# Cross-attention block: one 512-column V product per head group, one ring of eight PSUM banks, a rewritten order

## The chip, the core and the metric

The kernel runs on one core of a Trainium2 chip. The metric is the device time of one execution in microseconds; lower is better. The median of three runs before the change is 760.53 us (760.25 to 760.59).

PE is the matrix engine, with PEld for its weight loads; DVE, ACT and POOL are the vector, scalar and GpSimd engines; SP issues most of the DMAs. SBUF is the on-chip memory of the operands. PSUM holds what PE writes, in eight banks of 512 float32 values per partition.

## The reference

B = 4 batches, 512 queries and 512 context rows of width D = 512, H = 16 heads of HD = 32, a hidden layer of 2048, all in float32:

```python
x = layer_norm(hidden_states, ln1_w, ln1_b)
q = (x @ q_w + q_b).reshape(B, LQ, H, HD).transpose(0, 2, 1, 3)
k = (encoder_hidden_states @ k_w + k_b)...   # likewise, and v
scores = einsum('bhqd,bhkd->bhqk', q, k) / sqrt(HD)
scores = where(mask, scores, finfo.min)
out = einsum('bhqk,bhkd->bhqd', softmax(scores), v)
hidden = out.reshape(B, LQ, D) @ cproj_w + cproj_b + hidden_states
y = gelu(layer_norm(hidden, ln2_w, ln2_b) @ fc_w + fc_b)
return hidden + y @ proj_w + proj_b
```

## The kernel before

Everything is laid out transposed, with features on the partitions. The attention runs in 16 groups w = 0 to 15, four per batch; a group is four heads, 128 features. One more idea shapes the second half: the hidden layer's products are split into quarters by a Strassen-like scheme (sums on POOL and DVE, fewer products on PE).

The order of all work is written out by hand in the string ORDER. Each token names a generator; each time the token stands in the string the generator runs up to its next `yield`, and what it issues is appended to the engines' queues in that order. No scheduler moves anything afterwards; every engine works through its own queue, and waits where an operand or a buffer is not ready. The tokens that matter here:

- `k:w`, `q:w`, `v:w` make a group's K, Q and V: four products of 128x512 on all 128 rows and columns of the array (V: sixteen of 128x128), then ACT moves the result out of PSUM.
- `u:w:t` (`scores`, L510) is a *score unit*: four products, one per head, each on 32 rows of the array and all 128 columns, for 128 queries t against 512 keys. The four lie side by side in the array's rows and write four banks.
- `x:w:t` (`exps`, L518 and L521) takes the four banks in turn: DVE adds the mask, copies to SBUF and takes the minimum; ACT takes exp and its sum.
- `r:w:t` (`turn`, L529 to L539) transposes the tiles in 32x32 blocks on DVE into a buffer `tb`; `d` (`stay`, POOL) and `e` (`exchange`, twelve DMAs on SP) move the blocks to their partitions in the buffer `pT`. There are two `tb` and two `pT`, one for each half of the queries.
- `a:w:half` (`attend`, L568) is the *V product*: for 4 key tiles and 4 heads, sixteen products with all 128 rows and 32 columns of the array; four heads lie side by side in the columns. Each streams 256 columns, the queries of one half. DVE then multiplies by the reciprocal sums (L574).
- `c:b:t` is the output projection (L443), `s2`, `r2`, `n2`, `t2`, `y` the second layer norm and its sums, `f:b:c` the first hidden product (L621), `j` its joins on ACT and DVE (L646, L651, L330), `g` the gelu, `P`, `pj`, `J` the second hidden product with its joins, `so` the stores of the result, `lc`, `lx`, `lf`, `wk`, `wq`, `wv` loads.

A float32 product shows in the trace as two matmul records, so a score unit has 8 records, a V product 32, a K product 8. I call a row of products that use the array in the same shape a *stretch*: full-array (k, q, v, c, f, P and the transposes), score (32 rows) or V (32 columns).

PSUM before is divided: four banks `sc` belong to the score units, four banks `acc` go round in a ring (class Ring: `take` pops the bank that came free first, `done` appends it) for all other products. In the last batch's hidden layers, when the scores are over, half of the results go to `sc` instead.

Of the kernel before, what the change touches and what calls it, by code (L numbers as in the profile page):

```python
# [20 lines left out]
P = 128  # L21
# [5 lines left out]
NG = ND  # L27
# [33 lines left out]
s1:0 k:0 s1:0 s1:0 s1:0 r1:0 n1:0 n1:0 n1:0 n1:0 wq:1 wv:1 k:0 v:0 k:1 k:1 qb t1:0:1 t1:0:1 t1:0:0 t1:0:3 t1:0:0  # L61
  t1:0:2 m:0 t1:0:2 t1:0:3 q:0 q:0
u:0:0 x:0:0 x:0:0 x:0:0 x:0:0 q:1 r:0:0
u:0:1 r:0:0 lx:1 lf:0:0 lf:0:0 wq:2 wv:2 v:1 wk:3 wk:2 lx:1 lx:1 lc wv:3 lf:0:2 v:0 x:0:1 x:0:1 x:0:1 x:0:1 r:0:1
  r:0:1 q:1
u:0:2 r:0:1 r:0:1 q:2 x:0:2 x:0:2 x:0:2 x:0:2
u:0:3 r:0:2 x:0:3 x:0:3 v:1 x:0:3 v:3 x:0:3
u:1:0 k:3 v:2 e:0:0 e:0:0 e:0:0 lh:0 lh:0 wq:3 r:0:2 r:0:3 r:0:3 lx:1 wv:5 m:0 d:0:0 v:1 d:0:0 x:1:0 s1:1 r:0:3 r:0:3
  e:0:1 e:0:1 e:0:1 v:3 s1:1 x:1:0 x:1:0 x:1:0 r:1:0 r:1:0
u:1:1 k:2 x:1:1 x:1:1 x:1:1 v:2 x:1:1 k:2 r:1:1 s1:1  # L70
u:1:2 r:1:1 q:2 s1:1 x:1:2 x:1:2 x:1:2 x:1:2 k:3 d:0:1 d:0:1 v:0 fs:0:0 r:1:2 r:1:1 q:3
u:1:3 r1:1 a:0:0 ts:1 r:1:1 x:1:3 ts:1 le:1 wk:4 wq:4 wk:5 lt:1 lt:1 le:1 le:1 le:1 a:0:1 a:0:0 x:1:3 e:1:0 ts:1 k:4
  r:1:2 r:1:3 x:1:3 x:1:3 k:4
u:2:0 k:5 r:1:3 x:2:0 x:2:0 a:0:1 k:5 x:2:0 x:2:0 r:1:3
u:2:1 r:1:3 x:2:1 e:1:0 lb:1 e:1:0 lb:1 lt:1 lt:1 lf:0:1 wq:5 wk:6 wv:4 cb:0 d:1:0 v:2 d:1:0 d:1:1 x:2:1 q:3 r:2:0 v:5
  a:1:0 x:2:1 r:2:1 x:2:1
u:2:2 r:2:0 x:2:2 x:2:2 x:2:2 x:2:2 r:2:1 r:2:1 a:1:0 v:4
u:2:3 r:2:1 v:4 x:2:3 x:2:3 k:6 e:1:1 e:1:1 e:1:1 e:2:0 e:2:0 e:2:0 wv:7 d:1:1 na:1 wa:1 na:1 r:2:2 x:2:3 x:2:3 r:2:3
  r:2:3 wa:1 na:1 wa:1 na:1 d:2:0 a:1:1
u:3:0 r:2:2 k:6 wa:1 x:3:0 a:1:1 x:3:0 x:3:0 x:3:0 r:2:3 r:2:3 q:5  # L80
u:3:1 x:3:1 v:5 wv:6 e:2:1 e:2:1 e:2:1 wk:7 wq:7 d:2:0 r:3:0 q:5 x:3:1 x:3:1 x:3:1 v:5 d:2:1 r:3:0 r:3:1 r:3:1 r:3:1
  d:2:1 cb:0 v:3 a:2:0 v:7
u:3:2 q:4 x:3:2 x:3:2 x:3:2 x:3:2 q:4 a:2:0 r:3:1 lf:0:3 e:3:0 e:3:0 e:3:0
u:3:3 a:2:1 q:7 r:3:2 x:3:3 x:3:3 x:3:3 x:3:3
u:4:0 k:7 d:3:0 d:3:0 a:2:1 r:3:2 r:3:3 r:3:3 m:1 r:3:3 r:3:3 x:4:0 x:4:0 x:4:0 x:4:0
u:4:1 r:4:0 v:7 x:4:1 x:4:1 x:4:1 v:6 e:3:1 e:3:1 wv:9 e:3:1 lf:0:2 x:4:1 v:6
u:4:2 r:4:0 r:4:1 a:3:0 x:4:2 x:4:2 k:7 r:4:1 a:3:0 x:4:2 r:4:1 r:4:1 x:4:2 c:0:1 d:3:1 v:4 d:3:1
u:4:3 r:4:2 c:0:0 a:3:1 x:4:3 x:4:3 q:7 x:4:3 c:0:1 r:4:3 x:4:3 c:0:0
u:5:0 r:4:2 r:4:3 x:5:0 x:5:0 a:3:1 x:5:0 x:5:0 c:0:2
u:5:1 c:0:3 s2:0 r:4:3 wk:8 lh:0 d:4:0 cb:0 c:0:2 s2:0 s2:0 r:4:3 le:2 lx:2 le:2 lf:0:1 wq:6 s1:2 wk:9 lh:0 e:4:0  # L90
  e:4:0 e:4:0 le:2 le:2 c:0:0 v:7 fs:0:0 fs:0:0 cb:0 d:4:0 fs:0:1 x:5:1 c:0:3 fs:0:0 m:1 v:6 c:0:1 d:4:1 e:4:1 q:6
  wv:8 e:4:1 e:4:1 d:4:1 x:5:1 r:5:0 x:5:1 x:5:1 a:4:0
u:5:2 v:9 k:8 s2:0 r:5:0 x:5:2 r2:0 r:5:1 n2:0 r:5:1 n2:0 r:5:1 r:5:1 q:6 x:5:2 x:5:2 k:8 x:5:2 c:0:2 c:0:3 n2:0
u:5:3 a:4:0 n2:0 x:5:3 t2:0:1 t2:0:1 r:5:2 t2:0:0 t2:0:0 x:5:3 r:5:2 x:5:3 k:9 a:4:1 x:5:3 r:5:3 v:9 k:9 y:0
# [145 lines left out]
def xattn_block(ctx: ExitStack, tc: tile.TileContext, x, x_t, encT, mask, q_w, k_w, v_w, c_w, w_fc, p_w, vecs, rows, out):  # L240
# [679 lines left out]
```

## Time and profile before

| | us |
|---|---|
| median of three runs | 760.53 |
| profiled execution, span of its instructions | 758.0 |
| PE busy | 751.1 |
| DVE busy | 596.2 |
| ACT busy | 403.3 |
| POOL busy | 371.4 |
| PE's first matmul starts, its last ends (from the span's start) | 1.35, 754.62 |

The profiled execution's time of its own beyond the span is not among the numbers shown; the median of the runs lies 2.5 us over its span. Engines overlap, so the busy times do not add up to the span. A busy PE is a PE with a matmul in flight: the records overlap each other, so what a piece of work costs is read from the distance between the start of one record and the start of the next, not from a record's length. A merged row of the timeline gives the start of the first record, the time to the end of the last, and their count.

### The profile page before, as it was taken

The numbers are of one execution on the slowest core, as the hardware profiler recorded it, in microseconds if no ns is written. First come the engines' busy times: TensorE is split into PE (matmuls) and PEld (weight loads), VectorE is DVE, ScalarE is ACT, GpSimd is POOL, SyncE is SP. The second block draws the span as 40 slices with busy tenths as digits, with TensorE's granted clock in tenths as the row PEclk, the third lists the DMA queues.
The fourth block names the chain that finished last, engine by engine and source line by source line (L and its number), as shares of the span: only waits on it lengthen the run. The fifth ranks groups of instructions, "written<-read, shape, count | busy, mean of one in ns | idle before, by whom it ended". The sixth has DMA issues, their size and how long they took to land.

```text
span 758.0 us, 14114 instructions
## 1 busy us (share of the span) xinstructions
PE 751.1 (99%) x4925; PEld 534.0 (70%) x4925; DVE 596.2 (79%) x1209; ACT 403.3 (53%) x951; POOL 371.4 (49%) x401
## 2 busy tenths in 40 slices
PE   9999999999999999999999999999999999999998
PEld 6464555467665456665555677766888999999997
DVE  3798999999768888877778986644689799786982
ACT  2566766456777776778867686861343221211110
POOL 1155864743884656656757657854411022240232
PEclk9999999999999999999999999999999999999999
DMA  7698978877887898784977698789545648788575
GB/s 267 199 240 235 251 212 246 232 193 218 212 236 211 229 251 254 204 246 128 248 221 211 209 271 248 219 277 317 163 140 178 247 134 162 225 169 263 99 180 112
DMA packets 72133, 162.18 MB, mean 214 GB/s; under 512 B 11960, under 2 KB 24656, under 8 KB 70400
## 3 DMA queue, kind: packets, MB, share of 16 engines
q1 hardware_dynamic: 56864, 131.44, 59.7%
q0 software_dynamic: 15056, 29.84, 15.9%
q8 instruction: 39, 0.64, 0.4%
q14 instruction: 30, 0.25, 0.1%
q10 hardware_dynamic: 144, 0.02, 0.0%
HBM read 73.95 MB, written 25.18 MB: 131 GB/s over the span
## 4 chain that ended last, share of the span: by engine, by line
PE 96%; DVE 2%; DMA 1%; issue 0%; POOL 0%; ACT 0%; POOLq 0%; DVEq 0%
PE acc L621 37%; PE sc L621 11%; PE sc L510 9%; PE acc L475 8%; PE acc L487 8%; PE acc L443 7%; PE acc L568 7%; PE acc L497 7%; PE acc L369 1%; DMA pbt<-fc_w_dram 1%; PE acc L850 1%; DVE ext L333 0%; DVE swap L330 0%; DVE yT L330 0%; DVE xn L330 0%
## 5 line engine op out<-in xcount | busy, mean ns | idle before, releaser
L521 ACT ACTIVATE ptt<-ptt,mn 128x512 f32<-128x512 f32 x256 | 182.9, 716 | 78.0 <-DVE mn L518 77.5
L518 DVE CUSTOM_DVE_ANT_0 ptt<-sc,mix 128x512 f32<-128x512 f32 x256 | 164.6, 680 | 30.5 <-PE sc L510 29.1
L546 POOL COPY swap<-swap 32x1088 f32<-32x1088 f32 x128 | 139.8, 1092 | 70.0 <-DVE swap L539 43.9
L529 DVE STREAM_TRANSPOSE swap<-ptt 128x1024 f32<-128x1024 f32 x64 | 78.8, 1232 | 9.5 <-DMA pbt<-fc_w_dram 3.2
L536 DVE STREAM_TRANSPOSE swap<-ptt 128x1024 f32<-128x1024 f32 x64 | 78.3, 1224 | 1.8 <-ACT ptt L521 1.8
L510 PE MATMUL sc<-pbt 32*128 32x512 f32 x512 | 73.8, 640 | 0.8 <-ACT pbt L489 0.8
L669 POOL DMA_DIRECT2D gd<-st x32 | 24.4, 766 | 96.9 <-ACT st L667 87.0
L646 ACT COPY st<-acc 128x256 f32<-128x256 f32 x96 | 34.5, 368 | 69.6 <-PE acc L621 66.3
L497 PEld LDWEIGHTS acc<-ptt,ext 128*128 128x128 f32 x512 | 58.7, 192 | 8.7 <-issue 3.4
L621 PE MATMUL acc<-ys,wsum 128*128 128x256 f32 x256 | 64.1, 382 | 0.0
L568 PE MATMUL acc<-swap,mix 128*32 128x256 f32 x1024 | 61.6, 382 | 0.0
L497 PE MATMUL acc<-ptt,ext 128*128 128x128 f32 x512 | 60.8, 277 | 0.0
L646 ACT COPY xn<-acc 128x128 f32<-128x128 f32 x75 | 18.9, 270 | 77.4 <-PE acc L621 72.5
L621 PE MATMUL acc<-yT,pbt 128*128 128x256 f32 x240 | 58.9, 386 | 1.0 <-DVE mix L574 1.0
L475 PE MATMUL acc<-ext,ptt 128*128 128x512 f32 x128 | 59.1, 605 | 0.0
L487 PE MATMUL acc<-ext,ptt 128*128 128x512 f32 x128 | 58.4, 600 | 0.0
L443 PE MATMUL acc<-mix 128*128 128x512 f32 x128 | 58.0, 600 | 0.0
L621 PEld LDWEIGHTS acc<-yT,pbt 128*128 128x128 f32 x240 | 44.0, 190 | 19.7 <-issue 6.9
L621 PEld LDWEIGHTS acc<-ys,wsum 128*128 128x128 f32 x256 | 47.6, 190 | 12.0 <-POOL wsum L330 1.5
L568 PEld LDWEIGHTS acc<-swap,mix 128*32 128x32 f32 x1024 | 30.6, 109 | 31.4 <-issue 9.0
L330 DVE TENSOR_TENSOR st<-acc,st 128x512 f32<-128x512 f32 (+1 forms) x48 | 26.1, 544 | 32.0 <-ACT st L646 22.4
L521 ACT ACTIVATION_READ_ACCUMULATOR ptt<-ptt,mn 128x1 f32 x256 | 48.3, 189 | 0.0
(143 smaller groups left out, 1396.7 us busy)
## 6 DMA issues: line engine op xcount, KB each, us to landing
swap<-swap SPq DMA_DIRECT2D x384, 136.0 KB, 3.4
gd<-st POOLq DMA_DIRECT2D x32, 512.0 KB, 4.7
swap<-gd SPq DMA_DIRECT2D x12, 1024.0 KB, 5.8
pbt<-fc_w_dram SPq DMA_DIRECT2D x40, 256.0 KB, 4.3
xn<-x_dram SPq DMA_DIRECT2D x32, 256.0 KB, 5.3
ext<-fc_w_dram SPq DMA_DIRECT2D x24, 256.0 KB, 2.9
swap<-xn POOLq DMA_DIRECT2D x18, 256.0 KB, 4.7
ptt<-k_w_dram SPq DMA_DIRECT2D x16, 256.0 KB, 4.0
```

The costliest lines, as they stand in the source:

```text
L443: nc.tensor.matmul(acc, oT[:, g, ts(t, P)], wc[:, g, :], start=(g == 0), stop=(g == NG - 1))
L475: nc.tensor.matmul(acc, S["wk", w][:, d, :], eT[:, d, :], start=(d == 0), stop=(d == ND - 1))
L487: nc.tensor.matmul(acc, S["wq", w][:, d, :], xT[:, d, :], start=(d == 0), stop=(d == ND - 1))
L497: nc.tensor.matmul(acc[:, ts(t, P)], eT[:, d, ts(t, P)], S["wv", w][:, d, :], start=(d == 0), stop=(d == ND - 1),)
L510: nc.tensor.matmul(sc[h], S["qT", w][r, ts(qt, P)], S["kT", w][r, :], start=True, stop=True)
L518: nc.vector.tensor_tensor_reduce(out=s, in0=sc[h], in1=mb, scale=1.0, scalar=FMAX, op0=ALU.add, op1=ALU.min, accum_out=mn)
L521: nc.scalar.activation(s, s, AF.Exp, bias=mn, scale=-1.0, accum_out=S["sums", w][:, qt, h : h + 1])
L529: nc.vector.transpose(*two_heads[0])
L536: nc.vector.transpose(*two_heads[1])
L546: nc.gpsimd.tensor_copy(pT[ts(i, HD), i], tb[ts(i, HD), i])
L568: nc.tensor.matmul(av[ts(h, HD), : 2 * P].rearrange(shape, **kw), v[:, t, ts(h, HD)], p[t][h], start=(t == 0), stop=(t == NT - 1),)
L621: nc.tensor.matmul(o, x[:, k], y[:, k], start=(k == 0 and not more), stop=(k == n - 1), skip_group_check=more)
```

## The change

The V product is issued once per group with 512 columns over both `pT` buffers, in place of two halves with 256. To let its result lie in order, Q is written to SBUF with its queries permuted (`prep_q`), so that a score unit holds other 128 queries than before, and the final multiplication of `attend` runs once over 512 columns. The eight banks form one ring for everything: each product of a score unit takes a bank, and `exps` gives it back after DVE's pass; the hidden products do likewise. ORDER is a new text, with the same tokens but `a:w` for `a:w:half`.

```diff
 ORDER = """
...
-u:0:0 x:0:0 x:0:0 x:0:0 x:0:0 q:1 r:0:0
...
+u:0:0 wk:3 s1:1 lh:0 x:0:0 x:0:0
+u:0:1 x:0:1 x:0:1 x:0:0 r:0:0 x:0:0 x:0:1 x:0:1 v:1 k:1 q:2 v:1 r:0:0 cb:0 q:2 wv:3 lf:0:0
...
-    sc = [psum.tile([P, L], F32, tag=f"sc{h}", name=f"sc{h}") for h in range(HG)]
-    accs = Ring(psum.tile([P, D], F32, tag=f"acc{i}", name=f"acc{i}") for i in range(4))
+    accs = Ring(psum.tile([P, D], F32, tag=f"acc{i}", name=f"acc{i}") for i in range(8))
...
+    pT_all = swap[:, 2:4].rearrange("p k (i n) -> p (k i) n", i=NI)
...
-        nc.scalar.activation(qT, acc, AF.Identity, bias=qb[:, w % NG : w % NG + 1], scale=-scale)
+        o, i = qT.rearrange("p (t i q) -> p i t q", t=NT, i=NI), acc.rearrange("p (i t q) -> p i t q", t=NT, i=NI)
+        nc.scalar.activation(o, i, AF.Identity, bias=qb[:, w % NG : w % NG + 1], scale=-scale)
...
-            nc.tensor.matmul(sc[h], S["qT", w][r, ts(qt, P)], S["kT", w][r, :], start=True, stop=True)
+            sc = accs.take("s", w, qt, h)
+            nc.tensor.matmul(sc, S["qT", w][r, ts(qt, P)], S["kT", w][r, :], start=True, stop=True)
...
-                out=s, in0=sc[h], in1=mb, scale=1.0, scalar=FMAX, op0=ALU.add, op1=ALU.min, accum_out=mn
+                out=s, in0=accs.held["s", w, qt, h], in1=mb, scale=1.0, scalar=FMAX, op0=ALU.add, op1=ALU.min,
+                accum_out=mn,
             )
+            accs.done("s", w, qt, h)
...
-    def attend(w, half):
-        v, pT = S["v", w], pT_of[half]
-        av = accs.take("a", w, half)
...
+    def attend(w):
+        v = S["v", w]
+        av = accs.take("a", w)
+        p = pT_all[:, :, :PW].rearrange("p i (a t h q) -> p t h i a q", a=2, t=NT, h=HG)
         for t in range(NT):
             for h in range(HG):
                 nc.tensor.matmul(
-                    av[ts(h, HD), : 2 * P].rearrange(shape, **kw), v[:, t, ts(h, HD)], p[t][h],
+                    av[ts(h, HD), :].rearrange("p (i a q) -> p i a q", i=2 * NI, a=2), v[:, t, ts(h, HD)], p[:, t, h],
...
-        q = S["qc", b, c] = halves(sc[c % HG] if b == LAST else accs.take("qc", b, c))
+        q = S["qc", b, c] = halves(accs.take("qc", b, c))
...
-        q = S["qc", b, n, 2] = sc[LEVEL2.index((b, n)) % HG][:, :HL].rearrange("p (j n) -> p j n", j=2)
+        q = S["qc", b, n, 2] = accs.take("qc", b, n, 2)[:, :HL].rearrange("p (j n) -> p j n", j=2)
```

What moves is seen in the engines' queues. First PE, at the first scores. `sc_74` to `sc_77` and `acc_74` to `acc_81` are the banks, L487 (L484 after) is q, L497 (L495) is v, L510 (L509) a product of a score unit. Before:

```order
L487 MATMUL acc_79<-ext,ptt 128x512 x4
L510 MATMUL sc_74<-pbt 128x512
L510 MATMUL sc_75<-pbt 128x512
L510 MATMUL sc_76<-pbt 128x512
L510 MATMUL sc_77<-pbt 128x512
L487 MATMUL acc_78<-ext,ptt 128x512 x4
L510 MATMUL sc_74<-pbt 128x512
L510 MATMUL sc_75<-pbt 128x512
L510 MATMUL sc_76<-pbt 128x512
L510 MATMUL sc_77<-pbt 128x512
L497 MATMUL acc_81<-ptt,ext 128x128 x16
```

And now:

```order
L484 MATMUL acc_74<-ext,ptt 128x512 x4
L509 MATMUL acc_76<-pbt 128x512
L509 MATMUL acc_75<-pbt 128x512
L509 MATMUL acc_79<-pbt 128x512
L509 MATMUL acc_78<-pbt 128x512
L509 MATMUL acc_80<-pbt 128x512
L509 MATMUL acc_81<-pbt 128x512
L509 MATMUL acc_74<-pbt 128x512
L509 MATMUL acc_76<-pbt 128x512
L495 MATMUL acc_75<-ptt,ext 128x128 x16
L484 MATMUL acc_80<-ext,ptt 128x512 x4
```

Two score units stand in one stretch where a q stood between them; the second unit's last product and the v behind it write the banks of the first unit's first two products.

Second, PE at group 0's V product (L568 before, L565 after; L392 or L389 is a small transpose of statistics, L475 or L472 a k). Before:

```order
L510 MATMUL sc_77<-pbt 128x512
L568 MATMUL acc_80<-swap,mix 32x256 x16
L392 MATMUL acc_79<-ident,sx_502 8x128
L568 MATMUL acc_78<-swap,mix 32x256 x16
L475 MATMUL acc_79<-ext,ptt 128x512 x4
L510 MATMUL sc_74<-pbt 128x512
```

And now:

```order
L509 MATMUL acc_75<-pbt 128x512
L389 MATMUL acc_78<-ident,sx_479 8x128
L565 MATMUL acc_77<-swap,mix 32x512 x16
L509 MATMUL acc_81<-pbt 128x512
L509 MATMUL acc_80<-pbt 128x512
L509 MATMUL acc_74<-pbt 128x512
```

The two halves became one product of 512 columns, and score units follow it without a full-array product between. Over the whole queue of PE there are 70 full-array stretches, 64 score stretches and 30 V stretches before (two of them hold two V products), and 48, 47 and 16 now: 17 times two score units share a stretch. The counts of products other than the V products are the same.

Third, SP's queue at the end (`gd` holds the gelu's results, `xa` the sums after the projection, `out_dram` is the result). Before:

```order
L327 DMA st_88<-gd_98 128x1024
L327 DMA st_90<-gd_98 128x1024
L327 DMA out_dram<-yT 128x256 x2
L327 DMA yT<-xa_94 128x512 x4
L327 DMA swap<-gd_98 128x2048
L327 DMA out_dram<-swap 128x256 x8
L327 DMA out_dram<-yT 128x256 x8
```

And now:

```order
L324 DMA swap<-gd_98 128x2048
L324 DMA out_dram<-yT 128x256 x2
L324 DMA swap<-gd_98 128x2048
L324 DMA yT<-xa_94 128x512 x4
L324 DMA out_dram<-swap 128x256 x6
L324 DMA out_dram<-yT 128x256 x3
L324 DMA out_dram<-swap 128x256 x2
L324 DMA out_dram<-yT 128x256 x5
```

The result of the last product, batch 3's (3, 4), comes in two halves, each stored by one DMA. Before, the two are the last two rows of the last x8. Now the first half's store is the last of the x3, and two stores of batch 2 and four of batch 3 stand between it and the second half's, the very last.

More of the change, by code (lines that the diff above doesn't have):

```diff
@@ L70 @@
[L70 to L85, printed above, removed]
@@ L641, in fc, with joins @@
         product(q[:, 1], a[1][:, 2:4], t4, True)
-    def joins(g, key, own):
+    def joins(g, key):
         for i in (0, 2, 3):
@@ L654, in joins @@
         add(nc.vector, g[:, 2], q[:, 1], g[:, 2])
-        if own:
-            accs.done("qc", *key)
+        accs.done("qc", *key)
     def fc_join(b, c):
```

315 lines of the change are left out of this document (162 added, 153 removed).

## The prediction

> **What bounds the kernel now.** I read the page's busy times and clock first, then the chain of work that ended last, then PE's own waits, then PE's timeline for prices.
>
> ```profile
> span 758.0 us, 14114 instructions
> PE 751.1 (99%) x4925; PEld 534.0 (70%) x4925; DVE 596.2 (79%) x1209; ACT 403.3 (53%) x951; POOL 371.4 (49%) x401
> ...
> PEclk9999999999999999999999999999999999999999
> ...
> PE 96%; DVE 2%; DMA 1%; issue 0%; POOL 0%; ACT 0%; POOLq 0%; DVEq 0%
> ```
>
> PE is busy 99% of the span at full clock, and 96% of the chain is PE behind PE. So time is won by what PE does, and lost by what makes PE wait. It hardly waits now:
>
> ```profile
> PE acc L850 <- POOL nhalf L839: 1.4, 1, 1.4
> PE acc L621 <- DVE mix L574: 1.0, 1, 1.0
> PE sc L510 <- ACT pbt L489: 0.8, 1, 0.8
> PE acc L621 <- DVE ext L333: 0.2, 1, 0.2
> ```
>
> These four make 3.4 us. What remains is how dense PE's stream is. PE's timeline (start, length, records) shows it:
>
> ```profile
> 13.09 3.60 PE L475 MATMUL acc<-ext,ptt 128*128 128x512 f32 x8
> 16.53 2.16 PE L369 MATMUL acc<-ident,xn 128*128 128x128 f32 x16
> ...
> 23.98 3.70 PE L487 MATMUL acc<-ext,ptt 128*128 128x512 f32 x8
> 27.62 1.14 PE L510 MATMUL sc<-pbt 32*128 32x512 f32 x8
> ...
> 60.74 1.93 PE L568 MATMUL acc<-swap,mix 128*32 128x256 f32 x32
> 62.61 0.27 PE L392 MATMUL acc<-ident,sx 128*8 128x128 f32 x1
> 62.81 1.93 PE L568 MATMUL acc<-swap,mix 128*32 128x256 f32 x32
> 64.67 3.70 PE L475 MATMUL acc<-ext,ptt 128*128 128x512 f32 x8
> 68.31 1.14 PE L510 MATMUL sc<-pbt 32*128 32x512 f32 x8
> 69.38 3.70 PE L475 MATMUL acc<-ext,ptt 128*128 128x512 f32 x8
> ...
> 214.82 1.03 PE L621 MATMUL acc<-yT,wsum 128*128 128x256 f32 x4
> 215.68 1.03 PE L621 MATMUL acc<-ys,pbt 128*128 128x256 f32 x4
> ```
>
> Start to start, eight full-array records of 512 columns take 3.44 us among their like (13.09 to 16.53), so 0.43 each; the same eight ahead of a score unit take 3.64 (23.98 to 27.62, 64.67 to 68.31). Each change of the array's shape thus costs a full-array stretch 0.20 us. A score unit is two rounds of four records side by side, 2 x 0.43 = 0.86, and takes 1.07 (68.31 to 69.38): 0.21 more. A V product is eight rounds of 256 columns at 0.215 (0.86 for four, 214.82 to 215.68), 1.72, and takes 1.86 (62.81 to 64.67): 0.14 more.
>
> **What the change removes on PE.** The counts of stretches are from the two queues.
>
> - Full-array stretches, 70 to 48: 22 x 0.20 = 4.4. I take 4.2, since the short ones may have less to lose.
> - Score stretches, 64 to 47: 17 x 0.21 = 3.6. Two units in one stretch stand nowhere in the trace; the pair should take 1.07 + 0.86 = 1.93. From below the second unit pays its 0.21 again and the term is 0; from above it is 3.6. The nearest row is the full-array stretch, in which a record after the first costs 0.43 and nothing more, so I take 3.6.
> - V products. Now 32 x 1.86 less 2 x 0.14 for the two double stretches, 59.2. After, 16 of eight rounds of 512 columns: 16 x (8 x 0.43 + 0.14) = 57.3. Gain 1.9. This shape is not in the trace either. From below, a 512-column round costs two of 256 with a start of its own, the gain is 0; from above, if the start too goes, 4.1. The operand is read in runs of 32 values before and after, so I take 1.9.
>
> Sum: 4.2 + 3.6 + 1.9 = 9.7 us, between 4.2 and 12.1. The products themselves keep their counts and columns.
>
> The Trainium skill has a rule that speaks against the second term: "TensorE: Matmul & The Clock Gate", Part 3, The mechanism, says that a weight load overlaps matmuls in flight only where its row group is another. The second unit of a pair uses the first one's four row groups; by that rule its two loads would stand free, and the sum would be about 6.1. The eight records from 13.09 on use all rows and follow each other without a gap, so the trace does not bear the rule out, but has no 32-row case.
>
> **Off PE's path.** DVE's final multiplication runs 16 times over 512 columns for 32 times over 256:
>
> ```profile
> L574 DVE TENSOR_TENSOR mix<-acc,swap 128x256 f32<-128x256 f32 x32 | 13.2, 415 | 8.3 <-PE acc L568 8.2
> L330 DVE TENSOR_TENSOR xn<-acc,xn 128x512 f32<-128x512 f32 x16 | 10.8, 680 | 11.4 <-PE acc L443 11.4
> L489 ACT ACTIVATE pbt<-acc,qb 128x512 f32<-128x512 f32 x16 | 10.9, 680 | 8.4 <-PE acc L487 8.4
> ```
>
> 32 x 0.415 = 13.3 becomes 16 x 0.68 = 10.9: 2.4 us less of DVE, which hides it behind PE. Q's permuted write (L489) is ACT's, 53% busy; twice as long it would add 16 x 0.68 = 10.9 us to an engine with 355 us idle, 0.68 of it on PE's path, at the first score unit. I cost it at nothing.
>
> **What PE will wait for.** Three places.
>
> *The first pair of score units.* In the new queue the second unit's last product writes the first unit's first bank, and the v behind it the second. DVE's timeline shows when these come free:
>
> ```profile
> 24.07 0.69 DVE L518 CUSTOM_DVE_ANT_0 ptt<-sc,mix 128x512 f32<-128x512 f32 x1 [4.53 <-PE sc L510]
> ...
> 24.69 0.69 DVE L518 CUSTOM_DVE_ANT_0 ptt<-sc,mix 128x512 f32<-128x512 f32 x1
> ```
>
> The first score unit starts at 22.91 in the profile and would end at 24.84 as a pair. Its eighth product can't start before 24.07 + 0.69 = 24.76 and takes two rounds and a start, 1.07: it ends at 25.83, 1.0 us late. What is queued behind it on PE is that v and q:2, then the next pair. Bounds 0.5 (it starts as soon as the first pass of DVE lets it) and 2 (v waits again). I take 1.0.
>
> *From the first scores to the first hidden product.* Here PE has nothing but attention, DVE is nearly as long, and I compare their work stretch by stretch:
>
> ```profile
> 22.90:172.40 149.50, 149.49 (x977) 79.17 (x978) 139.22 (x311) 95.97 (x242) 84.89 (x83) 1.00 0.84 232
> 172.40:530.00 357.60, 356.42 (x2142) 226.05 (x2141) 270.25 (x581) 252.75 (x547) 231.19 (x258) 1.00 0.81 232
> ...
> 168.83 3.74 PE L497 MATMUL acc<-ptt,ext 128*128 128x128 f32 x32
> 172.40 1.03 PE L621 MATMUL acc<-yT,pbt 128*128 128x256 f32 x4
> ...
> DVE ptt L518 <- PE sc L510: 10.9, 14, 4.5
> DVE rsum L533 <- ACT ptt L521: 1.0, 1, 1.0
> DVE mix L574 <- PE acc L568: 0.8, 2, 0.5
> DVE ptt L518 <- DVE swap L529: 0.2, 1, 0.2
> ```
>
> The first two rows are windows (from and to, length, then busy time of PE, PEld, DVE, ACT, POOL), the next two PE's last v ahead of the first hidden product, 3.6 us from start to start; the waits are DVE's from 22.9 to 174.8. PE is full for 149.5 us; DVE works 139.2 and waits 10.9 for scores, 4.5 of it before the very first and 6.4 later, and 2.0 for other things. By the new queues PE's part up to the first hidden product has 8 score, 10 full-array and 5 V stretches less (1.7 + 2.0 + 0.7), one v less and one score unit more (-3.6 + 0.9): 7.1 us less, 142.4. DVE's has three passes of layer-norm statistics more (2.4) and otherwise the same: some 141.6, and it starts 1.2 late. So the two are equally long, and any wait of DVE now comes out as a wait of PE at the second layer norm of batch 0, `t2:0` or `y:0`, whose sums the first hidden products need. The pairs put eight banks ahead of DVE, so its 6.4 us for scores should shrink; I assume to 2, with the other 2.0 as before. As cover I count 2 us, half of the v that stands in the new queue between the first hidden products and the one that needs the sums: PE waits 2.0. Bounds 0 and 8 (all old waits stay). Later DVE has room: 357.6 us of PE against 270 of DVE from 172 to 530.
>
> *The end.*
>
> ```profile
> 751.00 3.62 PE L621 MATMUL acc<-ptt,swap 128*128 128x256 f32 x16
> ...
> 750.52 4.92 SPq L327 DMA_DIRECT2D out_dram<-yT  x8
> ...
> 754.66 0.42 DVE L330 TENSOR_TENSOR yT<-yT,acc 128x256 f32<-128x256 f32 x1 [2.05 <-PE acc L621]
> ```
>
> PE ends at 754.62, the last addition runs to 755.1 and the store lands at 758. In the new queue DVE adds the first half at about 1.7 before PE's end, then finishes another join, then SP issues four stores ahead of the last; at 4.92 / 8 = 0.6 us each they delay it by 1.5, at half of that by 0.4. I take 1.0.
>
> SP's queue at the start has the 1 MB of the projection's weights and three more rows of x ahead of the later weights. The first transfer that could be late is wq:2, which waits for the slot of q:0 before and after; I cost it at nothing, 1 us if the queue is full.
>
> **Sum.** 758.0 - 9.7 + 1.0 + 2.0 + 1.0 = 752.3 us of span, 5.7 less. The profiled execution's span lies 2.5 us under the median of the runs, and I carry that over: 760.5 - 5.7 = **754.8 us**.
>
> **Rivals.**
>
> 1. *Pairs of score units don't merge.* The second unit pays its start: 3.6 us back, 758.4. For it: no pair in the trace, and the skill's rule above. Against: full-array records at 0.43 without a gap.
> 2. *DVE's old waits all stay* before the first hidden product: PE waits 8 in place of 2, 760.8, no change that shows. For it: DVE's 10.9 us for scores in this stage. Against: eight banks ahead of it in place of four.
> 3. *Slower: DVE waits for ACT's exps between passes and transposes.* A pair lets DVE run its passes ahead, and the transposes, which need ACT's exp (716 ns in the row below), come sooner behind them. The place is the same stage, 100 passes and 24 turn units; if each turn unit waits for one exp, 24 x 0.72 = 17 us, and after 2 us of slack PE waits 15 in place of 2: 767.8. It decides from 24 x 0.33 = 8 us on. Against: this wait is 2.1 and 1.8 us in the whole run before, and the new queue of DVE alternates two units' tiles.
> 4. *The V product streams slower* with its eight blocks of operand than 0.43 per round: at 0.50, 16 x 8 x 0.07 = 9 us back, 763.8: the change then doesn't give what its fewer instructions say. Against: blocks of the same 32-value runs stream at full rate now.
>
> ```profile
> L521 ACT ACTIVATE ptt<-ptt,mn 128x512 f32<-128x512 f32 x256 | 182.9, 716 | 78.0 <-DVE mn L518 77.5
> L529 DVE STREAM_TRANSPOSE swap<-ptt 128x1024 f32<-128x1024 f32 x64 | 78.8, 1232 | 9.5 <-DMA pbt<-fc_w_dram 3.2 <-ACT ptt L521 2.1 <-POOL swap L546 2.0
> L536 DVE STREAM_TRANSPOSE swap<-ptt 128x1024 f32<-128x1024 f32 x64 | 78.3, 1224 | 1.8 <-ACT ptt L521 1.8
> ```
>
> **Chances.** The forecast 0.66, rival 1 0.10, rival 2 0.10, rival 3 0.09, rival 4 0.05. A measurement here tells 0.2%, 1.5 us, from no change. Faster than 759.0: the forecast, rival 1, and the milder parts of 2 and 4 (0.03 each), 0.82. Within: the rest of rival 2, 0.07. Slower: rivals 3 and 4, 0.11. The range runs from all of the 9.7 with a wait of 0.5 at the first pair and 1.5 less of the old waits (760.5 - 10.7 = 749.8) to 8 us of waits before the first hidden product with the other two at their lower bounds (760.5 - 9.7 + 8.9 = 759.7).
>
> **What would show it.** A pair of score units taking 1.93 us from start to start, a V product 3.58, PE's span between first and last record shorter by some 7; PE's waits naming DVE at L509 once near 24.8 and near the first hidden product, 3 us together; DVE's wait for scores well under the old 29 us; the last store issued later behind PE's end. Wrong would be: a pair near 2.14, rounds of the V product over 0.43, or PE waiting over 8 us before the first hidden product.

## The result, and the profile after

| | before | after |
|---|---|---|
| median | 760.39 (four runs, 759.61 to 760.59) | 777.66 (four runs, 776.95 to 778.63) |
| ratio, 95% interval | | 1.023 [1.0216, 1.0245] |
| profiled execution, span | 758.0 | 776.9 |
| first product of the hidden layer starts | 172.40 | 175.59 |

The forecast was 754.8 us, between 749.8 and 759.7. The kernel became 17 us slower.

The page of the kernel after: busy time of PE, the clock that TensorE was granted in 40 slices, and the shares of the chain of waits.

```profile
span 776.9 us, 12985 instructions
...
PE 760.1 (98%) x4413; PEld 529.1 (68%) x4413; DVE 611.2 (79%) x1193; ACT 394.2 (51%) x943; POOL 375.7 (48%) x401
...
PEclk9999999999999999999999999999899999999999
...
PE 64%; DVE 7%; SPq 1%; ACT 1%; issue 1%; DMA 1%; POOL 0%; DVEq 0%; POOLq 0%
```

PE issues 512 records fewer and is busy 9 us longer, and its share of the chain fell from 96% to 64%. "Busy 98%" hides this: a score stretch whose last product waits for a bank counts as busy, since the records ahead of it are in flight. So the waits are looked for in PE's timeline of the kernel after (start, length, records):

```profile
45.35 2.00 PE L509 MATMUL acc<-pbt 32*128 32x512 f32 x16
47.28 1.13 PE L472 MATMUL acc<-ext,ptt 128*128 128x512 f32 x2
...
124.66 4.33 PE L509 MATMUL acc<-pbt 32*128 32x512 f32 x16
128.92 5.34 PE L565 MATMUL acc<-swap,mix 128*32 128x512 f32 x32
...
182.96 1.35 PE L620 MATMUL acc<-yT,pbt 128*128 128x256 f32 x5 [1.70 <-DVE mn L517]
...
198.36 3.03 PE L509 MATMUL acc<-pbt 32*128 32x512 f32 x16
201.32 1.98 PE L472 MATMUL acc<-ext,ptt 128*128 128x512 f32 x4
...
553.69 0.30 PE L366 MATMUL acc<-ident,xn 128*128 128x128 f32 x1 [0.32 <-DVE xn L359]
556.64 3.95 PE L366 MATMUL acc<-ident,xn 128*128 128x128 f32 x15 [2.65 <-DVE xn L359]
560.38 1.91 PE L620 MATMUL acc<-yT,ext 128*128 128x256 f32 x4
```

The pair at 45.35 takes 1.93 us from start to start, as forecast; the one at 198.36 takes 2.96 and the one at 124.66 4.26. Of the 17 pairs, five take 1.93, three 2.6 to 2.7, six 2.96 and the others 3.07, 3.57 and 4.26. The last nine are the pairs in which one product of the second unit (two in the pair of 3.57 us) is given a bank that the first unit still holds, because a ninth bank's worth of results is not out of PSUM yet (followed through ORDER, the ring gives these nine, and no other pair, a bank of the pair's own first unit): at 2.96 three products of the second unit run side by side and the fourth runs alone behind them, 1.03 us. The nine together stand 28.7 us, 11.3 more than nine clean ones. At 556.64 PE waits for the last layer norm, and the transposes behind it run at half rate (15 records of 128 columns in 3.74 us; in the kernel before 16 take 1.91). The granted clock of these stretches (windows of the kernel after; the clock is the third number from the end) was 1.00 in the kernel before:

```profile
120.00:140.00 20.00, 20.00 (x102) 9.33 (x101) 17.74 (x39) 12.99 (x35) 7.95 (x8) 0.91 0.81 221
540.00:560.00 20.00, 17.02 (x67) 12.30 (x66) 17.79 (x26) 3.32 (x5) 14.32 (x19) 0.91 0.38 140
560.00:580.00 20.00, 20.00 (x92) 17.55 (x91) 16.65 (x28) 7.71 (x17) 3.19 (x4) 0.92 0.52 165
```

One more difference stands in the waits of SP's queue (line, releaser, us in total, times, longest). After:

```profile
SPq L324 <- DVE mix L573: 78.0, 14, 12.5
...
SPq L324 <- DVE swap L540: 12.8, 4, 6.5
```

and before:

```profile
SPq L327 <- DVE swap L539: 52.5, 17, 13.9
...
SPq L327 <- DVE mix L574: 26.2, 7, 5.7
```

These are the exchange's transfers. Those that wait for the V product's eviction (the final multiplication, `mix`) wait three times as long as before, and those that wait for VectorE's transposes of their own data (`swap`) a quarter. The sum grew little, from 79 to 91 us: what changed is that the exchange now follows the last V product and not its own data.

### The profile page after: what moved, and what is told of

The parts are those of the page before. It is cut to its first block, busy times and chain, and to the rows that moved or that the text cites. A ratio compares the mean times of both kernels' runs of the same rounds, so it can differ in the third digit from the quotient of the medians.

```text
span 776.9 us, 12985 instructions
## 1 busy us (share of the span) xinstructions
PE 760.1 (98%) x4413; PEld 529.1 (68%) x4413; DVE 611.2 (79%) x1193; ACT 394.2 (51%) x943; POOL 375.7 (48%) x401
## 4 chain that ended last, share of the span: by engine, by line
PE 64%; DVE 7%; SPq 1%; ACT 1%; issue 1%; DMA 1%; POOL 0%; DVEq 0%; POOLq 0%
PE acc L620 43%; PE acc L509 5%; PE acc L440 5%; PE acc L565 4%; PE acc L484 4%; PE acc L472 2%; SPq L324 1%; PE acc L495 1%; DVE swap L530 1%; DVE ptt L330 1%; DVE xn L359 1%; DVE ptt L517 1%; ACT ptt L522 1%; PE acc L366 1%; DVE swap L537 1%
## 5 line engine op out<-in xcount | busy, mean ns | idle before, releaser
L517 DVE CUSTOM_DVE_ANT_0 ptt<-acc,mix 128x512 f32<-128x512 f32 x256 | 164.1, 680 | 38.5 <-PE acc L509 35.1
L547 POOL COPY swap<-swap 32x1088 f32<-32x1088 f32 x128 | 142.2, 1111 | 67.3 <-DVE mix L573 37.8
L530 DVE STREAM_TRANSPOSE swap<-ptt 128x1024 f32<-128x1024 f32 x64 | 78.7, 1232 | 8.5 <-ACT ptt L522 3.2
L509 PE MATMUL acc<-pbt 32*128 32x512 f32 x512 | 82.3, 629 | 1.5 <-ACT pbt L487 1.5
L537 DVE STREAM_TRANSPOSE swap<-ptt 128x1024 f32<-128x1024 f32 x64 | 77.7, 1216 | 0.5 <-ACT ptt L522 0.4
L495 PEld LDWEIGHTS acc<-ptt,ext 128*128 128x128 f32 x512 | 58.9, 192 | 8.8 <-DVE mn L517 4.1
L565 PE MATMUL acc<-swap,mix 128*32 128x512 f32 x512 | 59.9, 610 | 1.7 <-POOL wsum L327 1.4
L495 PE MATMUL acc<-ptt,ext 128*128 128x128 f32 x512 | 60.6, 277 | 0.1
L472 PE MATMUL acc<-ext,ptt 128*128 128x512 f32 x128 | 58.8, 602 | 0.7 <-DMA ptt<-k_w_dram 0.7
L327 DVE TENSOR_TENSOR st<-acc,st 128x512 f32<-128x512 f32 (+1 forms) x64 | 34.9, 547 | 30.7 <-ACT st L645 19.7
L665 ACT ACTIVATE st<-st,vec 128x512 f32<-128x512 f32 x64 | 44.2, 719 | 28.4 <-DVE st L327 28.0
L484 PE MATMUL acc<-ext,ptt 128*128 128x512 f32 x128 | 57.9, 596 | 0.1
L509 PEld LDWEIGHTS acc<-pbt 32*128 32x128 f32 x512 | 27.6, 183 | 40.7 <-issue 15.9
```

What stands on the lines that cost most here:

```text
L472: nc.tensor.matmul(acc, S["wk", w][:, d, :], eT[:, d, :], start=(d == 0), stop=(d == ND - 1))
L484: nc.tensor.matmul(acc, S["wq", w][:, d, :], xT[:, d, :], start=(d == 0), stop=(d == ND - 1))
L495: nc.tensor.matmul(acc[:, ts(t, P)], eT[:, d, ts(t, P)], S["wv", w][:, d, :], start=(d == 0), stop=(d == ND - 1),)
L509: nc.tensor.matmul(sc, S["qT", w][r, ts(qt, P)], S["kT", w][r, :], start=True, stop=True)
L517: nc.vector.tensor_tensor_reduce(out=s, in0=accs.held["s", w, qt, h], in1=mb, scale=1.0, scalar=FMAX, op0=ALU.add, op1=ALU.min, accum_out=mn,)
L530: nc.vector.transpose(*two_heads[0])
```

## The experiments

All times are medians, the ratios are against the kernel before on the same chip. In the excerpts of ORDER "..." leaves tokens out. The short name in brackets stands for the run from there on. TensorE, VectorE, ScalarE, GpSimd and SyncE are other names of PE, DVE, ACT, POOL and SP.

### Banks

Nine pairs taken apart (s9; here the first):

```diff
-u:0:0 wk:3 s1:1 lh:0 x:0:0 x:0:0
-u:0:1 x:0:1 x:0:1 x:0:0 r:0:0 x:0:0 x:0:1 x:0:1 v:1 k:1
+u:0:0 wk:3 s1:1 lh:0 x:0:0 x:0:0 x:0:0 r:0:0 x:0:0 v:1
+u:0:1 x:0:1 x:0:1 x:0:1 x:0:1 k:1
```

> The changed kernel, with nine pairs of score units taken apart: the next token of TensorE is put between the two units, in those nine pairs whose second unit gets a bank that the first unit still holds. The bank theory: these nine pairs took 11.3 us more than nine clean pairs of 1.93 us; taken apart they cost the pairs' gain (9 x 0.2 us = 1.9 us), and the half-rate stretch after the 4.26 us pair near 130 us (1.7 us) should go too: 777.7 - 11.3 + 1.9 - 1.7 = 766.6, range 765 to 770. The rival, that VectorE's passes set the pace of the score stages whatever the banks are: the wait only moves behind the unit, 775 to 778.

Measured: 780.87, 1.0271 [1.0253, 1.0288], slower than the change as it was and than both forecasts. Five of the nine, from 198 us on, lost all or most of their wait. In front of that it came back elsewhere: three pairs that were left together grew by 0.6 to 0.9 us each. The pair of 4.26 us kept its wait; PE's timeline of this kernel:

```profile
125.71 1.14 PE L507 MATMUL acc<-pbt 32*128 32x512 f32 x8
129.54 5.34 PE L563 MATMUL acc<-swap,mix 128*32 128x512 f32 x32 [2.69 <-DMA ptt<-k_w_dram]
```

The unit now runs clean in 1.07 us, and the V product behind it still starts at 129.54 and not at 126.8: another wait stood behind the bank's, at the same place. The profile puts it down to a load of K's weights, which the V product does not read. The exchange fits better: its last transfer for this product goes out at 126.59, and in the four kernels in which PE stands idle ahead of this product (s9 and k3, dva, sd below) the product starts 2.93 to 2.95 us after that transfer, in the kernel after 3.3.

Three evictions earlier (k3: k:1, k:4, k:7; here the third):

```diff
-u:4:2 r:4:1 x:4:2 x:4:2 r:4:1 r:4:1 r:4:2
-u:4:3 ... wk:9 r:4:2 k:7 wv:8
+k:7
+u:4:2 r:4:1 x:4:2 x:4:2 r:4:1 r:4:1 r:4:2
+u:4:3 ... wk:9 r:4:2 wv:8
```

> The changed kernel with TensorE's order as it is; only the ScalarE evictions of three K products (w = 1, 4, 7) are moved ahead of the pair of score units they stood behind, so that their banks are back in the ring before the pair's second unit takes its four. The bank theory: these three pairs (2.96, 3.07 and 4.26 us) become 1.93 us each, 4.5 us less, and the half-rate stretch behind the third (1.7 us) goes with it: 771.5, range 770.5 to 773.5. The rival (VectorE sets the pace): 776 to 778.

Measured: 777.16, 1.0219 [1.0202, 1.0236]: no gain. The first pair now takes 1.93, but the second 3.65 and the third 4.97. The third's last product goes out at 128.7, behind k's eviction, to which ACT comes only behind three exps and the evictions of v and q (ACT's timeline of this kernel):

```profile
126.21 0.70 ACT L519 ACTIVATE ptt<-ptt,mn 128x512 f32<-128x512 f32 x1
...
126.92 0.56 ACT L497 COPY mix<-acc 128x512 f32<-128x512 f32 x1
127.39 0.68 ACT L484 ACTIVATE pbt<-acc,qb 128x512 f32<-128x512 f32 x1
127.97 0.68 ACT L471 ACTIVATE pbt<-acc,vec 128x512 f32<-128x512 f32 x1
```

And then the V product waits for the exchange as well (PE's timeline):

```profile
125.70 4.11 PE L506 MATMUL acc<-pbt 32*128 32x512 f32 x16
130.67 3.64 PE L562 MATMUL acc<-swap,mix 128*32 128x512 f32 x32 [0.85 <-DMA swap<-swap]
```

The ring of eight alone, with the order and the V halves of before (b8):

```diff
-    sc = [psum.tile([P, L], F32, tag=f"sc{h}", name=f"sc{h}") for h in range(HG)]
-    accs = Ring(... for i in range(4))
+    accs = Ring(... for i in range(8))
```

> One part of the change alone: the order before, with two V products per w, but all eight banks in one ring for scores and everything else. If the ring itself is harmless: 760, range 758 to 762, since the order before never puts two units side by side and so asks for no more than it did. The rival, that handing banks round in one ring is what makes TensorE wait: 766 or more.

Measured: 763.96, 1.0049 [1.0031, 1.0066], between the two forecasts. The ring alone costs 3.4 us, without a pair in the order. From the first record of each of the 64 score stretches to the record behind it, they take 3.5 us more than before together.

The same with another rule for which bank is handed out (rb8):

```diff
+RELEASED = """... s:0:0:0 s:0:0:1 s:0:0:2 s:0:0:3 v:0 ..."""
...
+    def done(self, *key):
+        ...
+        self.free.append(b)
+        self.free.sort(key=lambda b: self.at[id(b)])
...
-    accs = Ring(... for i in range(8))
+    accs = Banks(... for i in range(8))
```

> The order before with all eight banks in one ring (763.96 us, 3.4 us slower than the kernel before, 3.5 us of it in score stages), but the ring hands out the bank that was freed first by the clock of that kernel's trace instead of the one whose release stands first in program order. If a bank is late only because program order says nothing of when an engine gets to it: the 3.4 us go, 759 to 761.5. The rival, that eight banks in common are one too few at those places, whichever is chosen: 762.5 to 765.

Measured: 760.99, 1.0005 [0.9992, 1.0018]: the ring's cost is gone. The bank that stands first in program order is not the one that is free first; two engines evict, each in its own order, and the text does not say which of them gets to its eviction first.

### VectorE

Half of the transposes of w = 1 to 7 left out, in the kernel after (dva) and in the kernel before (dvb):

```diff
-        nc.vector.transpose(*two_heads[0])
+        if not 1 <= w <= 7:
+            nc.vector.transpose(*two_heads[0])
```

> The changed kernel without the first of the two VectorE transposes of each score unit for w = 1 to 7 (the probabilities of two heads are left out of the result there): 28 x 1.16 = 32 us less VectorE work between about 45 and 235 us, TensorE's order untouched. The theory that VectorE, 92% busy from 60 to 220 us, is what TensorE runs into there: the 7.5 us that the changed kernel falls behind in this stage go, 768 to 772. The rival (banks held by other products, ScalarE's evictions): 775 to 778.

Measured: 779.19, 1.0247 [1.0217, 1.0278]: no gain, though DVE's busy time (third of the busy times) in the stage fell by 26 us, as these windows show, first after, then without the transposes:

```profile
60.00:220.00 160.00, 156.59 (x839) 84.22 (x832) 146.70 (x311) 102.22 (x256) 98.30 (x98) 0.99 0.83 223
```

```profile
60.00:220.00 160.00, 155.04 (x837) 84.05 (x830) 120.47 (x288) 101.16 (x254) 96.98 (x96) 0.98 0.83 223
```

> The kernel before with the same 28 transposes left out (same part of the result missing). If TensorE is the bound there and VectorE only keeps up with it: no more than the 2 us that TensorE waits in this stage, 758.5 to 760.5. The rival, that VectorE bounds the kernel before in this stage too: 753 to 757.

Measured, in the kernel before: 758.9, 0.9979 [0.9965, 0.9992], 1.7 us, as expected. VectorE alone sets the pace in neither kernel.

### The exchange

In the kernel after, SP's exchange of w = 2, the evictions and the V products of w = 1 to 3 (grouped rows of the source views: shortest, median and longest ns, then the first and last start in us):

```profile
L324 SPq DMA_DIRECT2D swap<-swap x24: 518/589/1299, 87.3 to 102.5; - x24
```

```profile
L573 DVE TENSOR_TENSOR mix<-acc,swap x3: 691/692/692, 86.6 to 134.3; 128x512 f32<-128x512 f32 x3
```

```profile
L565 PE MATMUL acc<-swap,mix x96: 592/592/1061, 82.9 to 133.7; 128*32 128x512 f32 x96
```

The first V product starts at 82.9 and is evicted from 86.6 to 87.3; at 87.3 the first of 24 transfers goes out, the last at 102.5; the next V product starts at 106.0. This loop has a turn of 23 us. Before, each half had a loop of its own, and while one half was being exchanged the other was used. Now one product reads both buffers, and all 24 transfers of the next group stand behind its eviction. All 15 first transfers go out within 1.2 us of it. But only five of the 15 V products behind the first (w = 1, 2, 3, 6 and 15) start less than 4 us after the last transfer; for the others it is 6 to 15 us, so that the loop can hold them up less or not at all.

Two thirds of the transfers left out, in the kernel after (xa) and in the kernel before (xb):

```diff
         for d in range(1, NI):
-            for i in (0, 2, 1, 3):
+            for i in (0, 2, 1, 3) if w == 0 or d == 1 else ():
```

> The changed kernel with 16 of the 24 transfers that exchange a w's probabilities left out for w = 1 to 15 (the result is wrong there); all orders untouched. New theory, the exchange loop: the single V product reads both halves, so the next w's transfers can only start at its eviction (in the changed kernel each of the 15 first transfers goes out within 1.2 us of that eviction), SyncE needs 15 to 27 us to issue all 24, and the next V product waits for the last; three bare turns of this loop (V products at 59.2, 82.9, 106.0, 128.9 us) take 23 us each. With 8 transfers a turn is 10 us shorter, so the loop binds nowhere: 760 to 768. The rival, that VectorE's and ScalarE's own order makes TensorE wait and the loop only runs along: 774 to 778.

Measured: 775.2, 1.0212 [1.0186, 1.0239], against 1.023 for the whole change: no gain that can be told, and not the 760 to 768 of the loop theory. PE's timeline at the same place as above:

```profile
123.99 4.34 PE L506 MATMUL acc<-pbt 32*128 32x512 f32 x16
128.26 3.64 PE L562 MATMUL acc<-swap,mix 128*32 128x512 f32 x32
```

Now the exchange is early (its last transfer goes out 9.5 us ahead), and the pair's banks hold the V product at 128.26.

> Control: the kernel before with the same 16 of 24 transfers left out. Its two halves are loops of their own, with 4 to 25 us between the last transfer's issue and the product. The loop theory: no more than 1.5 us, 758.5 to 761. The rival, that fewer transfers help any kernel by taking load off the queue: as much gain as in the changed kernel, over 5 us.

Measured: 757.45, 0.9965 [0.9954, 0.9976]: 2.8 us, a little more than the theory gave and well under the rival's 5. So much of a gain from leaving transfers out is common to both kernels.

The V product alone, in the order of before (bv):

```diff
-    def attend(w, half):
+    def attend(w):
...
-u:2:0 ... a:0:1 ... u:2:1 x:2:1 e:1:0 lb:1 e:1:0
+u:2:0 ... a:0 ... e:1:0 ... e:1:0 ... e:1:0
```

> The kernel before with one part of the change alone: one V product of 512 columns per w, at the place of the old second half, with four banks for the scores and four in the ring as before; transfers of the next w's first half and the output products of the last w of a batch stand behind it, since they need its banks and buffers free. If the V product itself is harmless: 16 products of 3.58 us for 32 of 1.86 us, 2.2 us less, against the first halves that now go out later: 758, range 756 to 762. The rival, that the single product is what costs (it makes both halves wait for the later exchange): 766 to 775.

Measured: 899.9, 1.1811 [1.1774, 1.1848]. The forecast of this run was off by 140 us. In this order the second halves stand late, so all of the next group's exchange starts late, and SP waits for the eviction

```profile
SPq L324 <- DVE mix L570: 190.9, 15, 23.8
```

for 190.9 us, with all that stands behind it in SP's queue. It does not show the loop alone: PE's own waits name VectorE, ScalarE and a weight load, the V products start 4.5 us or more after the last transfer, and the granted clock was 0.93 on average. What it shows is that a rewritten order was needed for the single V product at all.

The V product in halves again, in the new order (av2; here w = 1):

```diff
-... x:2:2 x:2:1 k:5 x:2:1 ... r:2:2 r:2:2 r:2:1 lt:1 na:1 wq:4 k:4 wk:6 a:1 a:1
+... x:2:2 a:1:0 x:2:1 k:5 a:1:0 x:2:1 ... r:2:2 r:2:2 r:2:1 d:2:0 d:2:0 e:2:0 e:2:0 e:2:0 lt:1 na:1 wq:4 k:4 wk:6 a:1:1 a:1:1
```

> The changed kernel with the V product taken apart again into two halves of 256 columns, nothing left out: the second half stays where the single product stands, the first half goes some 9 us of TensorE's work ahead of it (for w = 2 and 10 just ahead of it, for want of a bank), and the transfers of the next w's first half follow the first half's eviction. The loop theory: the turn is broken at most places, 32 halves cost 2 us more than 16 products, the waits shrink: 766 to 773. The rival, that the loop only runs along: 778 to 781.

Measured: 886.73, 1.1677 [1.1645, 1.171]. It tells nothing of the loop: PE's longest waits in it are for weights,

```profile
PE acc L475 <- DMA ptt<-k_w_dram: 40.4, 4, 13.1
```

whose loads stand on SP behind the transfers that I had moved ahead of them.

### Two and three at once

Every single edit of the new order so far, other than av2, left 775 to 781 us. The next kernels combine the edits shown above: all three (cmb), pairs and transposes (sd), pairs and transfers (sx).

> The changed kernel with three suspects taken away at once, each of which alone left the time as it was: the nine pairs apart (as in the first experiment), 28 VectorE transposes left out for w = 1 to 7, and 16 of 24 exchange transfers left out for w = 1 to 15 (the result is wrong where they are missing). New theory, side by side: banks, VectorE's queue and the exchange hold the same places, so that one gives way to the next; together the 15 us of waits in score stages shrink to 2 or so, the half-rate stretch at 130 us goes, and nine more stretches cost 3.8 us: 766, range 763 to 770. The rival, that something none of them touches sets the time: 773 or more.

Measured: 769.45, 1.0116 [1.0101, 1.0131]: 8 us less than the change, within the range of the theory.

> Two of the combined kernel's three edits: the nine pairs apart and the 28 VectorE transposes left out, all exchange transfers kept. If the wait of the pairs taken apart goes to VectorE's queue, this alone gives most of the combined kernel's gain: 769 to 772. If the exchange loop is what takes it over: 776 to 781. If all three are needed: 774 or more here and in the other of these two runs.

Measured: 777.54, 1.0224 [1.0196, 1.0251].

> The other two: the nine pairs apart and 16 of 24 exchange transfers left out, all VectorE transposes kept. If VectorE's queue takes over the pairs' wait: 775 to 780. If it is the exchange loop: 769 to 772.

Measured: 772.93, 1.0173 [1.0149, 1.0196]. This is a microsecond over the range given for the exchange, and two under VectorE's. So it is mostly the exchange that takes over from the banks: with the pairs apart, leaving transfers out gains 7.9 us (780.87 to 772.93), and with the pairs together 2.5. VectorE's transposes gain 3.3 us with the pairs apart (780.87 to 777.54) and 3.5 with the transfers gone too (772.93 to 769.45), and nothing with the pairs together. So the banks hid both, and these two hardly hide each other. The kernel before gains 2.8 and 1.7 us from the same omissions; the change's own share is nearer to 5.1 and 1.6. Of the 7.9 us, 5.2 are there at the V product of w = 4 (165.96 in s9, 160.78 in sx). PE's timeline shows the exchange just ahead of it. Pairs apart and fewer transposes:

```profile
124.27 1.14 PE L507 MATMUL acc<-pbt 32*128 32x512 f32 x8
128.99 4.96 PE L564 MATMUL acc<-swap,mix 128*32 128x512 f32 x32 [3.58 <-DMA swap<-swap]
```

Pairs apart and fewer transfers:

```profile
124.51 1.14 PE L507 MATMUL acc<-pbt 32*128 32x512 f32 x8
125.58 3.64 PE L563 MATMUL acc<-swap,mix 128*32 128x512 f32 x32
```

The V product of w = 3 starts at 128.9 in the kernel after, at 129.5, 128.3 and 128.9 with one edit each (pairs, transfers, transposes), at 129.0 with the first and the last, and at 125.6 only when both its banks and its exchange are out of the way.

### The last layer norm

The last loads earlier (ln3):

```diff
-e:15:1 e:15:1 e:15:1 lf:3:0 lp:5 ... c:3:1 lp:7 lh:3 lh:3
+lh:3 lh:3 e:15:1 e:15:1 e:15:1 lf:3:0 lp:5 ... c:3:1 lp:7
```

> The changed kernel with the last two loads of x for the second LayerNorm of batch 3 moved ahead of the last exchange of the probabilities on SyncE's queue. If these loads hold the chain GpSimd bias, VectorE sum, statistics, normalisation, the 4.9 us that TensorE waits between 553 and 558 us shrink by about 2.5 us and the half-rate stretch behind them (3.3 us) shortens: 772 to 775. The rival: the four output products of batch 3 behind the last V product set this chain, not the loads: 776.5 to 778.

Measured: 778.26, 1.0239 [1.0215, 1.0263]: no gain. The transposes start at 553.51 and, behind 2.66 us of waiting, at 556.47, as before the edit.

VectorE's sums over the projection weights later (lnp):

```diff
-a:15 c:3:0 ps:4 c:3:1 ... cb:3 ps:4 ps:4 c:3:2 ... n2:3 n2:3
+a:15 c:3:0 c:3:1 ... cb:3 c:3:2 ... n2:3 n2:3 ps:4 ps:4 ps:4 ...
```

> The changed kernel with nine tokens of VectorE's sums over the projection weights moved from between the last output products and the second LayerNorm of batch 3 to behind that LayerNorm. If they hold up the chain of sums, statistics and normalisation: the 4.9 us that TensorE waits at 553 to 558 us go and the half-rate stretch behind them (3.3 us) too, 769 to 773. The rival, that the chain is as long without them: 776 to 778.

Measured: 780.29, 1.0258 [1.0226, 1.0289]: no gain. The wait at the transposes is gone, and the sums now stand in front of the layer norm's results:

```profile
551.64 1.91 PE L363 MATMUL acc<-ident,xn 128*128 128x128 f32 x16
553.55 0.70 PE L617 MATMUL acc<-yT,ext 128*128 128x256 f32 x2
560.03 4.21 PE L617 MATMUL acc<-yT,ext 128*128 128x256 f32 x9 [5.79 <-DVE yT L371]
```

Both (lnx):

> The changed kernel with the two edits at the last LayerNorm together: the last two loads of x go ahead of the last exchange, and all of VectorE's sums over projection weights go behind the LayerNorm and the four sums over its result. Each edit alone left the time as it was. If the two chains are of equal length, so that each hides the gain of the other: TensorE's 4.9 us of waits and the half-rate stretch behind them go, 770 to 774. The rival, that the last V product, set by the exchange loop, fixes this stage: 776 to 778.

Measured: 780.96, 1.0282 [1.0259, 1.0304], 3.3 us slower than the change. The wait moved once more, to the hidden product whose join stands on VectorE behind the sums:

```profile
554.89 1.91 PE L363 MATMUL acc<-ident,xn 128*128 128x128 f32 x16
...
571.01 2.07 PE L617 MATMUL acc<-ys,ext 128*128 128x256 f32 x4 [5.22 <-DVE st L324]
```

So the sums are no obstacle that can be pushed back; they have to be done earlier. There is room: in the kernel after, VectorE (third busy time) works 5 of the 20 us around the last V product, which starts at 527 us. It waits for that product and then for the output products behind it:

```profile
520.00:540.00 20.00, 20.00 (x88) 11.21 (x87) 5.25 (x9) 3.18 (x5) 1.55 (x2) 1.00 0.99 334
```

Loads and sums earlier (tl):

```diff
-e:15:1 e:15:1 e:15:1 lf:3:0 lp:5 ... lp:1 ... a:15 j:2:5 lp:3 a:15 c:3:0 ps:4 ... lh:3 lh:3 ... ps:4 ps:4 ... ps:0 ps:0
+lp:5 lp:1 lp:3 lh:3 lh:3 e:15:1 e:15:1 e:15:1 lf:3:0 ... a:15 j:2:5 ps:4 ps:4 ps:4 ps:0 ps:0 a:15 c:3:0 ...
```

> The changed kernel with the stage of batch 3's last LayerNorm put in another order: three loads of projection weights and the last two loads of x go ahead of the last exchange on SyncE, and five of VectorE's sums over projection weights go ahead of the eviction of the last V product, into the 15 us that VectorE stands idle before it. If it is VectorE's queue together with the loads behind the exchange that makes TensorE wait at 553 to 558 us: 4.9 us of waits and the 3.3 us half-rate stretch behind them shrink to a third or less, 770 to 774. The rival, that the chain from the last V product (output products, sums, statistics) is that long by itself: 776 to 781.

Measured: 774.0, 1.0182 [1.0157, 1.0207]. This is the only single edit of the change whose gain can be told from its scatter, 3.7 us, at the edge of the expected range. Of the waits at the layer norm hardly anything is left, and the transposes run at full rate:

```profile
547.62 7.07 PE L617 MATMUL acc<-pbt,swap 128*128 128x256 f32 x32
554.53 2.24 PE L363 MATMUL acc<-ident,xn 128*128 128x128 f32 x16
556.76 2.90 PE L617 MATMUL acc<-yT,ext 128*128 128x256 f32 x12
```

Everything together (all):

> The three suspects of the combined kernel and the new order at the last LayerNorm together. If these account for the loss: 757 to 764, about the time of the kernel before. If something else holds it: 768 or more.

Measured: 765.01, 1.006 [1.0045, 1.0075], a microsecond over the range. Of the 17.3 us, 12.6 are gone, though up to 4.5 of them are the gain that leaving work out gives the kernel before as well (1.7 and 2.8 us above). The rest was not taken apart. PE's timeline of the kernel after has five waits behind the first hidden product, at 183, 323, 342, 442 and 516 us, that cost 1.9, 1.6, 1.4, 0.9 and 1.3 us from start to start; the kernel with everything together still has them all, 7.2 us, and no run touched their causes. No version faster than the kernel before came out of this; the ring by release time with the old order (760.99) is even with it.

## Why the prediction was wrong

**What PE's stream costs: right.** A pair without a wait takes 1.93 us (forecast 1.93) and a V product 3.57 (3.58). Rivals 1 and 4 fall with that. By the weight-load rule of the Trainium skill ("TensorE: Matmul & The Clock Gate", Part 3, The mechanism) the pair would be 2.14; the five clean pairs do not show it. The prediction says that its trace has no 32-row case, but every score unit is one: in the unit at 27.62 us the four loads of the second round run from 27.72 to 27.93, beside the first round's matmuls in the same row groups (27.62 to 28.32).

With these prices (0.43 us for 512 columns, a quarter of it where four records run side by side, and 0.20, 0.21 and 0.14 us for each full-array, score and V stretch) all of PE's stretches add up to 736.5 us before and 726.6 after, 9.9 us less for a forecast of 9.7. What the trace takes beyond that, waits and half rate, is in us:

| stage of PE's queue | before | after | everything together |
|---|---|---|---|
| up to the first score unit | 4.0 | 3.6 | 4.0 |
| up to the first hidden product | 0.9 | 11.3 | 4.5 |
| up to the last V product | 4.6 | 17.7 | 12.7 |
| from there to PE's end | 7.3 | 12.9 | 7.3 |
| sum | 16.8 | 45.5 | 28.5 |

**"What PE will wait for. Three places": the step that failed.** It counts 1.0 and 2.0 us, and 1.0 at the end; even the upper end of the range has room for 8.9 us. By the table 28.7 came, 13.1 of them between the first hidden product and the last V product, where the prediction counts nothing. Each of its parts:

- *The first pair's bank, 1.0 us.* The mechanism and size were right (2.96 for 1.93), the count was wrong: it was read from one excerpt of the queue, and eight more pairs have it. Together 11.3 us instead of 1.0, and s9 shows that five of them came off when the units stood apart, though it was no faster for it. To count them would have taken no trace, only the ring followed through ORDER.
- *"The pairs put eight banks ahead of DVE, so its 6.4 us for scores should shrink."* DVE's wait for scores in the whole run grew to 35.1 us, from 29 (costliest groups of the page after):

```profile
L517 DVE CUSTOM_DVE_ANT_0 ptt<-acc,mix 128x512 f32<-128x512 f32 x256 | 164.1, 680 | 38.5 <-PE acc L509 35.1
...
L530 DVE STREAM_TRANSPOSE swap<-ptt 128x1024 f32<-128x1024 f32 x64 | 78.7, 1232 | 8.5 <-ACT ptt L522 3.2
...
L537 DVE STREAM_TRANSPOSE swap<-ptt 128x1024 f32<-128x1024 f32 x64 | 77.7, 1216 | 0.5 <-ACT ptt L522 0.4
```

  The eight banks are not ahead of DVE: they belong to everyone, and b8 and rb8 show that sharing them in program order costs 3.4 us even without pairs.
- *From the first scores to the first hidden product, 2.0 us.* Forecast was PE's first hidden product at 22.6 + 142.4 + 3.0 = 168.0, and it starts at 175.6, with another wait of 1.7 us at 183. Rival 2 allowed 8 us here, so its size was nearer, but its reason, VectorE's old waits, was not: with VectorE 26 us less busy in this stage (dva) it starts at 175.0. In the score stretches up to there 7.8 us are lost, 5.5 of them in four of the nine pairs, and 1.7 in the V product at half rate. The runs with two edits put the price on banks and the exchange, of which the one hid the other.
- *The exchange is missing.* The prediction costs the V product's columns and DVE's multiplication, and says nothing of the buffers that the product frees. s9, xa and sx show at the V product of w = 3 that the loop of product, eviction and 24 transfers takes over where the banks let go. That it does so elsewhere is not shown.
- *"Later DVE has room."* That was said of 172 to 530 us, and is true of the mean, 270 of 357.6 us before. But PE lost 13.1 us more in this stage, 5.8 in the banks of five pairs and 7 in the five waits named above. Behind it, at the last layer norm, the prediction looks at nothing: VectorE stands idle until the last V product and has the projection's sums and the layer norm to do behind it. PE's waits there, 3.3 us from start to start, and as much again at half rate were in no term. tl shows their place: without them the last stage is back at 7.3 us.

**The end, +1.0: wrong.** From PE's end to the span's it is 3.4 us in both kernels. The four other stores have gone out before the last addition is done.

**Rival 3** (VectorE waits for ACT's exp): before the transposes (L530 and L537 above) this wait is 3.2 and 0.4 us in the whole run after, 3.6 together for 3.9 before. It does not decide.

## What to carry to other kernels

A buffer that two steps used in halves is a pipeline: count what a single use of both delays, by following the product, its eviction and the next fill as one loop and comparing the turn with what lies between. A common ring should hand out what is free first by the clock, and a change that asks for more buffers at once has to be followed through the whole order, not at its first place. When one suspect after another can be removed without any gain, look at one place on the time line and remove two: the start of one product, compared across the runs, told here which wait stood behind which.

## What was not expected of the hardware

The clock that was granted fell behind some stretches of PE and not behind others of the same length. Behind 2.69 us of waiting in s9 the V product of w = 3 took 5.34 us, and behind 3.58 us in sd 4.96; in k3, behind a pair of 4.97 us in which products trickled out one at a time, the same product ran at full rate, 3.64. In the kernel after it stands behind a pair of 4.26 us and takes 5.34 at a granted clock of 0.68; in xa it stands behind one of 4.27 us and takes 3.64 at 1.00. Nor is it fixed by the kernel: the mean clock was 0.993 to 0.996 in the four executions of the kernel after and 0.993 to 0.998 in those of k3. So the 1.7 us of half rate at 130 us need not be a steady part of the change's price. What decides was not tried.
